# Attention in a two-layer graph network: scores and values on four 64x64 tiles, a new order of the pieces, channel means by DMA

## The chip, the cores and the metric

One core of a Trainium2 chip. The metric is the device time of one execution in microseconds (us), the median over several runs. All runs quoted here of one kernel lie within 0.2% of each other. In profiles PE is TensorE, PEld its weight loads, DVE is VectorE, ACT is ScalarE, POOL is GpSimd; L569 is a line of the kernel.

## The reference, cut to what matters

The first layer (a normalised graph product and two dense layers) is untouched by the change. The second layer is this, for 16 batches of 1024 nodes, 256 channels and 4 heads, all float32:

```python
c_adj = mean(x, channels)                      # one number per node
A   = 2 * | |sigmoid(c_j - c_i) - 0.5| - 0.5 |
g   = relu((x^T @ (adj * A)) * para)           # the queries q
k, v = x @ kv_w                                # 4 heads of 64 channels
attn = softmax(q k^T * scale)
out  = layernorm(x + attn @ v)
```

Of the kernel before, what the change touches and what calls it, by code (L numbers as in the profile page):

```python
# [9 lines left out]
F32 = mybir.dt.float32  # L10
# [3 lines left out]
PSUM = bass.MemoryType.PSUM  # L14
DRAM = bass.MemoryType.DRAM

P = 128
# [5 lines left out]
def gnn_norm_attention_kernel(  # L23
# [16 lines left out]
    nc = tc.nc  # L40
    B, N, C = x.shape
    H = W1.shape[0]
    NT = N // P
    CT = C // P
    HT = H // P
    FB = 512
    NH = N // FB
    HD = C // HEADS
# [3 lines left out]
    dram = ctx.enter_context(tc.tile_pool(name="dram", bufs=1, space=DRAM))  # L52
    ctx.enter_context(tc.manual_schedule())

    ident = const.tile([P, P], F32, name="ident")
# [22 lines left out]
    yT_all = dram.tile([B, P, CT, N], F32, name="yT")  # L78
    yT_dram = [yT_all[b] for b in range(B)]

    LDP = 2
    s2 = const.tile([P, CT], F32, name="s2")
    t2 = const.tile([P, CT], F32, name="t2")
# [2 lines left out]
    with ExitStack() as l0:  # L86
# [29 lines left out]
        with ExitStack() as ph1:  # L116
# [9 lines left out]
            for i in range(0, NT, 2):  # L126
                t = hp.tile([P, 2, N], F32, tag="h", name=f"A{i}")
# [29 lines left out]
            for h in range(NH):  # L157
# [11 lines left out]
                for j in range(NT):  # L169
                    p = ps.tile([P, FB], F32, tag="ah"[j % 2], name="pat")  # L170
# [25 lines left out]
            for c in range(HT):  # L196
                p = ps.tile([P, FB], F32, tag="a", name="pw1")
# [3 lines left out]
            for c in range(CT):  # L201
                p = ps.tile([P, FB], F32, tag="a", name="pw2")
# [90 lines left out]
            for b in range(B + 1):  # L293
                if b < B:
                    aggregate(b)
                if b > 0:
                    for h in range(NH):
                        u = (b - 1) * NH + h
                        hT[u] = hp.tile([P, HT, FB], F32, tag="h", name=f"hT{u}")
                        for f in range(HT):  # L300
                            p = hidden(b - 1, h, f)
# [34 lines left out]
        with ExitStack() as ph2:  # L336
# [3 lines left out]
            order = list(range(len(units) - KEEP, len(units))) + list(range(len(units) - KEEP))  # L340
# [68 lines left out]
    def fast():  # L409
      with ExitStack() as fx:  # L410
        pool = lambda name, bufs, **k: fx.enter_context(tc.tile_pool(name=name, bufs=bufs, **k))
        x1p = pool("x1p", 11)
        x1Tp = pool("x1Tp", 1)
        crp = pool("crp", 1)
# [8 lines left out]
        rp = pool("rp", 2)  # L423
        ps_s = pool("ps_s", 2, space=PSUM)
        ps_o = pool("ps_o", 1, space=PSUM)
        ps_t = pool("ps_t", 3, space=PSUM)

        x1s, x1Ts, css, crows, mvs, wgs = {}, {}, {}, {}, {}, {}
        kTs, qTs, vs, S, E, ACC, O, OT, DT = {}, {}, {}, {}, {}, {}, {}, {}, {}
# [44 lines left out]
            hcs[b] = sm.tile([P, NT], F32, tag="hcs", bufs=2, name=f"hcs_{b}")  # L474
            nc.vector.tensor_scalar_mul(hcs[b], css[b], 0.5)

        def crow(b, h):

            if h == 0:
                crows[b] = crp.tile([P, N], F32, tag="crow", name=f"crow_{b}")  # L480
            p = ps_t.tile([P, FB], F32, tag="t", name="pc")
            for k in range(FB // P):
                j = h * (FB // P) + k
                nc.tensor.transpose(p[:, ts(k, P)], css[b][:, j : j + 1].to_broadcast([P, P]), ident)
            nc.scalar.copy(crows[b][:, ts(h, FB)], p)


        def wg_a(b, i):
# [53 lines left out]
                nc.vector.tensor_scalar(qs, qs, 0.0, scale, op0=OP.max, op1=OP.mult)  # L542


        def step(g):
            b, s = divmod(g, NS)
            hf, pair, cp = s // (NP * NT // 2), s // (NT // 2) % NP, s % (NT // 2)
            return b, hf, pair, cp

        def scores(g):  # L550
            b, hf, pair, cp = step(g)
            for a in range(2):
                cb = 2 * cp + a
                t = ps_s.tile([P, 2, FB], F32, tag="s", name=f"s{g}_{a}")
                for h in range(2):
                    nc.tensor.matmul(  # L556
                        t[:, h, :],
                        kTs[b, pair][h * HD : (h + 1) * HD, ts(cb, P)],
                        qTs[b, pair, hf][h * HD : (h + 1) * HD, :],
                        start=True,  # L560
                        stop=True,
                    )
                S[g, a] = t

        def exps(g):
            for a in range(2):
                E[g, a] = ep.tile([P, 2, FB], F32, tag="e", name=f"e{g}_{a}")
                nc.scalar.activation(E[g, a], S.pop((g, a)), AF.Exp)  # L568

        def sums(g):  # L570
            b, hf, pair, cp = step(g)
            if cp == 0:
                ACC[b, hf, pair] = accp.tile([P, 2, FB], F32, tag="acc", name=f"acc{g}")
                nc.vector.tensor_add(ACC[b, hf, pair], E[g, 0], E[g, 1])  # L574
            else:
                for a in range(2):
                    nc.vector.tensor_add(ACC[b, hf, pair], ACC[b, hf, pair], E[g, a])  # L577

        def attend(g):
            b, hf, pair, cp = step(g)  # L580
            if cp == 0:
                O[b, hf, pair] = ps_o.tile([P, FB], F32, tag="o", name=f"o{g}")
            for a in range(2):
                cb = 2 * cp + a
                for h in range(2):
                    nc.tensor.matmul(  # L586
                        O[b, hf, pair][h * HD : (h + 1) * HD, :],
                        vs[b][:, cb, pair * P + h * HD : pair * P + (h + 1) * HD],
                        E[g, a][:, h, :],
                        start=(cb == 0),  # L590
                        stop=(cb == NT - 1),
                    )
                E.pop((g, a))
            if cp == NT // 2 - 1:
                t = otp.tile([P, FB], F32, tag=f"ot{pair}", bufs=2 - pair, name=f"ot{g}")
                nc.scalar.copy(t, O.pop((b, hf, pair)))
                OT[b, hf, pair] = t

        def dens(b, hf):
# [82 lines left out]
        NC = NS // 2  # L682
        at = {}

        def put(w, t, f, *a):
            at.setdefault(w * NC + t, []).append((f, a))

        WG = (3, 3, 1, 1)
        KV = (3, 3, 2)
        QG = (6, 6, 6, 7, 7)  # L690
        for b in range(B):

            for hf in range(NH):
                t = (hf + 1) * (NC // NH)
                put(b, t, dens, b, hf)
                put(b, t + 1, recips, b, hf)
                for k in range(KB // 2):
                    put(b, t + 1 + k, finish_a, b, hf * (KB // 2) + k)
                    put(b, t + 2 + k, finish_b, b, hf * (KB // 2) + k)

            put(b - 2, 2, begin, b)
            for j in range(NT // 2):
                if b > 0 or j >= LDP:
                    put(b - 2, j, load, b, j)
                put(b - 2, j + 1, bn2, b, j)
                put(b - 2, j + 2, ln1_a, b, j)
                put(b - 2, j + 3, ln1_b, b, j)
                put(b - 2, j + 4, x1_t, b, j)
            put(b - 2, NC - 2, means, b)
            for h in range(NH):  # L710
                put(b - 2, NC - 1, crow, b, h)

            i = 0
            for t, n in enumerate(WG):
                for i in range(i, i + n):
                    put(b - 1, t, wg_a, b, i)
                    put(b - 1, t, wg_b, b, i)
                i += 1
            kv = [(keys, (b, c, h)) for c in range(CT) for h in range(NH)]
            kv += [(values, (b, j)) for j in range(0, NT, 2)]  # L720
            for t, n in enumerate(KV):
                for _ in range(n):
                    f, a = kv.pop(0)
                    put(b - 1, t, f, *a)
            m = 0
            for t, n in enumerate(QG):
                for m in range(m, m + n):
                    put(b - 1, NC - len(QG) + t, graph, b, m)
                m += 1
# [3 lines left out]
        nsteps = B * NS  # L733
# [3 lines left out]
        rank = {f: k for k, f in enumerate(order)}  # L737
        short = (dens, recips, finish_a, x1_t, ln1_a, crow)
        long = (keys, values, graph)

        def arrange(pieces):
            few = sorted((fa for fa in pieces if fa[0] not in long), key=lambda fa: rank.get(fa[0], 11))
            many = [fa for fa in pieces if fa[0] in long]
            n = sum(f in short for f, _ in few)
            res, k, done = [], 0, 0
            for f, a in few:
                res.append((f, a))
                if f in short and f is not dens:
                    k += 1
                    upto = len(many) * k // n  # L750
                    res += many[done:upto]
                    done = upto
            return res + many[done:]

        for t in range(min(at), max(max(at), nsteps // 2 - 1) + 1):
            g = 2 * t
            now = arrange(at.get(t, []))
            live = [k for k in (g, g + 1) if 0 <= k < nsteps]
            ahead = [k for k in (g + 2, g + 3) if 0 <= k < nsteps]
            if ahead:  # L760
                scores(g + 2)
                exps(g + 2)
            while now and now[0][0] is dens:
                f, a = now.pop(0)
                f(*a)
            if live:
                sums(g)
            if not now and live:
                attend(g)
                live.pop(0)  # L770
                sums(g + 1)
            for f, a in now:
                f(*a)
            if now and live:
                sums(g + 1)
            if ahead:
                scores(g + 3)
                exps(g + 3)
            for k in live:
                attend(k)  # L780

        return nc.values_load(
            badi[0][0:1, 0:1],
# [3 lines left out]
        )  # L787

    flag = fast()


# [149 lines left out]
```

## The kernel before: the parts that the change touches

The second layer is one software pipeline. A batch has eight *turns* of two *steps*. A turn scores two steps (`s`, then exps on ScalarE), multiplies two earlier steps with the values (`o`), and between them does *pieces* that finish the batch before (`pd`, `pr`, `pf`), prepare the next (gate rows `wg`, keys `pk`, values `pv`, queries `pg`) and normalise the one after (`py`, `px`, means `pc`).

```python
ps_s = pool("ps_s", 2, space=PSUM)     # two tiles of two banks for scores
ps_o = pool("ps_o", 1, space=PSUM)     # one bank
ps_t = pool("ps_t", 3, space=PSUM)     # three banks for all the short-lived tiles
...
def scores(g):                         # 64 rows x 128 columns, two row tiles
    for h in range(2):
        nc.tensor.matmul(t[:, h, :], kTs[b, pair][h*HD:(h+1)*HD, ts(cb, P)],
                         qTs[b, pair, hf][h*HD:(h+1)*HD, :], start=True, stop=True)
def attend(g):                         # 128 rows x 64 columns, two column tiles
    for h in range(2):
        nc.tensor.matmul(O[h*HD:(h+1)*HD, :], vs[b][:, cb, ...64 columns...],
                         E[g, a][:, h, :], start=(cb == 0), stop=(cb == NT - 1))
def crow(b, h):                        # means of all nodes along every partition
    for k in range(FB // P):
        nc.tensor.transpose(p[:, ts(k, P)], css[b][:, j:j+1].to_broadcast([P, P]), ident)
    nc.scalar.copy(crows[b][:, ts(h, FB)], p)
... (cut)
for t in turns:                        # the order within a turn
    scores(g + 2); exps(g + 2)
    sums(g)                            # softmax denominators, VectorE
    for f, a in now: f(*a)             # the pieces
    sums(g + 1)
    scores(g + 3); exps(g + 3)
    attend(g); attend(g + 1)
```

## Time and profile before

| | before |
|---|---|
| time, median | 2702.65 us |
| TensorE busy | 97% of the span |
| VectorE, ScalarE busy | 51%, 45% |
| one batch in steady state | 113.03 us |
| waits of TensorE in it | 2.0 us |

"Busy" of TensorE includes the modelled tails of pipelined matmuls (593 ns for one of pg, where the next starts 0.43 us after it), so it hides the cost of a change of tile shape. What shows it is the distance from the start of one run of matmuls to the start of the next.

### The profile page before, as it was taken

To read this page: it belongs to the slowest core of one execution; us is meant where nothing else is said; L and a number is where in the kernel's file an instruction comes from. 1 tells how busy PE (TensorE), PEld (TensorE's weight loads), DVE (VectorE), ACT (ScalarE), POOL (GpSimd) and SP (SyncE) were. 2 spreads that over 40 slices of the span, in tenths; PEclk is the share of its full clock that TensorE was granted. 3 is DMA by queue.
4 is the path that set the end of the run, shared out by engine and by line. 5 is a ranking of instruction groups with operands and counts; after the bars stand their busy time and mean duration, and the time that the engine had idled before them with its cause. 6 is when DMAs were issued, how large, how long until landed. Compare 5 with 4: busy or idle time off the path is not lost.

```text
span 2701.5 us, 24578 instructions
## 1 busy us (share of the span) xinstructions
PE 2632.3 (97%) x9186; PEld 1127.8 (42%) x9186; DVE 1386.3 (51%) x2198; ACT 1223.3 (45%) x1650; POOL 259.5 (10%) x464
## 2 busy tenths in 40 slices
PE   8999999999998999999999999999999999999997
PEld 4444444444443444443444444344444443444432
DVE  5222222223213465665656656576565765657646
ACT  2111111114554555464554645546455464654634
POOL 1110111100000000100101001010000100001002
PEclk9999999999998999999999999999999999999999
DMA  3222122122863100010000100001000010000000
GB/s 125 94 78 78 78 94 88 72 106 93 319 218 109 32 16 24 28 43 24 24 24 28 43 24 24 24 28 43 24 24 24 28 43 24 24 24 28 12 8 25
DMA packets 91389, 153.18 MB, mean 57 GB/s; under 512 B 7296, under 2 KB 73344, under 8 KB 84352
## 3 DMA queue, kind: packets, MB, share of 16 engines
q1 hardware_dynamic: 91264, 151.55, 16.0%
q8 instruction: 74, 1.21, 0.2%
q14 instruction: 51, 0.42, 0.1%
HBM read 89.66 MB, written 61.87 MB: 56 GB/s over the span
## 4 chain that ended last, share of the span: by engine, by line
PE 90%; DVE 5%; ACT 3%; issue 1%; POOL 0%; DMA 0%; SPq 0%; ACTq 0%; DVEq 0%; POOLq 0%
PE s L556 16%; PE pg L536 16%; PE o L586 15%; PE pa L262 13%; PE po L360 8%; PE ph L283 8%; PE pk L510 4%; PE pv L521 3%; DVE wg L502 1%; PE px L469 1%; PE pd L605 1%; PE pa L246 1%; PE py L446 1%; PE pf L627 1%; DVE acc L577 1%
## 5 line engine op out<-in xcount | busy, mean ns | idle before, releaser
L568 ACT ACTIVATE e<-s 128x1024 f32<-128x1024 f32 x512 | 497.7, 1021 | 599.6 <-PE o L586 351.7
L556 PE MATMUL s<-qT,kT 64*128 64x512 f32 x2048 | 509.7, 616 | 17.4 <-ACT e L568 17.4
L577 DVE TENSOR_TENSOR acc<-acc,e 128x1024 f32<-128x1024 f32 x384 | 469.7, 1223 | 19.6 <-DVE acc L577 1.4
L536 PE MATMUL pg<-wg,x 128*128 128x512 f32 x1024 | 470.3, 593 | 0.6 <-DVE wg L502 0.6
L586 PE MATMUL o<-e,v 128*64 128x512 f32 x2048 | 467.7, 598 | 0.0
L556 PEld LDWEIGHTS s<-qT,kT 64*128 64x128 f32 x2048 | 174.8, 186 | 327.2 <-issue 192.2
L302 ACT COPY hT<-ph 128x512 f32<-128x512 f32 x128 | 75.0, 586 | 453.7 <-PE ph L283 453.7
L586 PEld LDWEIGHTS o<-e,v 128*64 128x64 f32 x2048 | 135.5, 136 | 316.5 <-issue 315.4
L536 PEld LDWEIGHTS pg<-wg,x 128*128 128x128 f32 x1024 | 180.2, 190 | 160.6 <-issue 159.2
L283 PE MATMUL ph<-agg,W1T 128*128 128x512 f32 x512 | 222.2, 592 | 0.0
L502 DVE SCALAR_TENSOR_TENSOR wg<-wg,adj_sb 128x1024 f32<-128x1024 f32 x128 | 156.8, 1225 | 77.4 <-ACT wg L498 73.9
L360 PE MATMUL po<-hL,W2T 128*128 128x512 f32 x432 | 185.6, 592 | 0.0
L303 DVE BATCH_NORM_STATS2 st<-ph 128x6 f32<-128x512 f32 x128 | 89.5, 699 | 136.6 <-ACT hT L302 136.6
L262 PE MATMUL pa<-T,sx 128*128 128x512 f32 x360 | 156.9, 592 | 0.0
L574 DVE TENSOR_TENSOR acc<-e,e 128x1024 f32<-128x1024 f32 x64 | 78.2, 1222 | 153.0 <-PE pd L605 153.0
L283 PEld LDWEIGHTS ph<-agg,W1T 128*128 128x128 f32 x512 | 97.3, 190 | 122.5 <-issue 122.2
L541 DVE TENSOR_TENSOR qT<-pg,para_sb 128x512 f32<-128x512 f32 x64 | 44.2, 691 | 203.0 <-PE pg L536 203.0
L66 POOL TENSOR_SCALAR rs_z<-mv_z 128x2 f32<-128x2 f32 x64 | 17.5, 274 | 1194.1 <-DVE mv_z L401 1041.6
L364 DVE BATCH_NORM_STATS2 st<-po 128x6 f32<-128x512 f32 x64 | 44.8, 699 | 169.3 <-PE po L360 169.3
L521 PE MATMUL pv<-kvw,x1T 128*128 128x256 f32 x512 | 119.4, 382 | 6.6 <-DVE r L630 6.6
L360 PEld LDWEIGHTS po<-hL,W2T 128*128 128x128 f32 x432 | 82.1, 190 | 103.3 <-issue 103.3
L510 PE MATMUL pk<-x1T,kvw 128*128 128x512 f32 x256 | 117.8, 603 | 0.6 <-ACT kT L513 0.6
(130 smaller groups left out, 2450.5 us busy)
## 6 DMA issues: line engine op xcount, KB each, us to landing
h<-hT SPq DMA_DIRECT2D x27, 1024.0 KB, 3.8
hL<-h SPq DMA_DIRECT2D x27, 1024.0 KB, 6.2
x<-in_x_dram SPq DMA_DIRECT2D x16, 1024.0 KB, 5.2
yT<-y SPq DMA_DIRECT2D x32, 512.0 KB, 3.7
yt<-yT SPq DMA_DIRECT2D x64, 256.0 KB, 3.6
xr<-in_x_dram SPq DMA_DIRECT2D x64, 256.0 KB, 3.6
out_dram<-r SPq DMA_DIRECT2D x64, 256.0 KB, 2.1
A<-in_adj_dram SPq DMA_DIRECT2D x4, 1024.0 KB, 7.9
```

The lines of the kernel that those rows point to most:

```text
L262: nc.tensor.matmul(p, w[:, k, :], m[:, k, :], start=(k == 0), stop=(k == KN - 1))
L283: nc.tensor.matmul(p, W1T[:, k, ts(f, P)], aggT[b][:, k, ts(h, FB)], start=(k == 0), stop=(k == CT - 1),)
L303: nc.vector.bn_stats(st1[:, f, u, :], p)
L360: nc.tensor.matmul(po[c], W2T[:, k, ts(c, P)], hT[u][:, k, :], start=(k == 0), stop=(k == HT - 1))
L502: nc.vector.scalar_tensor_tensor(t, t, 1.0, adj_sb[:, i, :], op0=OP.add, op1=OP.mult)
L510: nc.tensor.matmul(p, kvw[:, k, ts(c, P)], x1Ts[b][:, k, ts(h, FB)], start=(k == 0), stop=(k == CT - 1))
L521: nc.tensor.matmul(p[:, ts(a, C)], x1Ts[b][:, k, ts(j + a, P)], kvw[:, k, C:], start=(k == 0), stop=(k == CT - 1),)
L536: nc.tensor.matmul(pg[b], x1s[b, k // 2][:, k % 2, ts(c, P)], wgs[b, k][:, ts(h, FB)], start=(k == 0), stop=(k == NT - 1))
L556: nc.tensor.matmul(t[:, h, :], kTs[b, pair][h * HD : (h + 1) * HD, ts(cb, P)], qTs[b, pair, hf][h * HD : (h + 1) * HD, :], start=True, sto ...
L568: nc.scalar.activation(E[g, a], S.pop((g, a)), AF.Exp)
L577: nc.vector.tensor_add(ACC[b, hf, pair], ACC[b, hf, pair], E[g, a])
L586: nc.tensor.matmul(O[b, hf, pair][h * HD : (h + 1) * HD, :], vs[b][:, cb, pair * P + h * HD : pair * P + (h + 1) * HD], E[g, a][:, h, :], ...
```

## The change

Its intent: 64x64 tiles let scores and values share one tile shape, so that a turn can run s, o, s, o as one stretch without the *edges* between shapes. (An edge is the time that TensorE loses when a run of matmuls in one tile shape follows a run in another, 0.14 to 0.20 us in the kernel before; a *slot* is the 0.43 us from one 128x128 matmul of 512 columns to the next.) For this, each pair of products becomes four small ones, o takes two PSUM banks, one for each row tile, and the short-lived tiles lose a bank. The turn is reordered: pieces first, then s, o, s, o; sums behind the last short piece; two gate rows in each of four turns; pieces spread among each other. Scores now run one step less ahead of the values that use them. The channel means go out to memory and come back broadcast.

```diff
-        ps_t = pool("ps_t", 3, space=PSUM)
+        ps_t = pool("ps_t", 2, space=PSUM)
 ... crow
+            nc.tensor.transpose(p[:NT, :P], css[b], ident)
+            t = crows[b][:NT, :P]
+            nc.scalar.copy(t, p[:NT, :P])
+            nc.sync.dma_start(c_dram[b], t)
+            nc.sync.dma_start(crows[b], c_dram[b].rearrange("j p -> (j p)").partition_broadcast(P))
 ... scores (attend alike, with row tile r into bank r of o)
+                for r in range(2):
+                    for h in range(2):
+                        nc.tensor.matmul(t[r * HD : (r + 1) * HD, h, :],
+                            kTs[b, pair][h * HD : (h + 1) * HD, ts(2 * cb + r, HD)],
+                            qTs[b, pair, hf][h * HD : (h + 1) * HD, :], start=True, stop=True)
 ... end of attend
+                nc.scalar.copy(t, o[:, 0, :])
+                nc.vector.tensor_add(t, o[:, 1, :], t)
 ...
-        WG = (3, 3, 1, 1)
+        WG = (2, 2, 2, 2)
 ... arrange: pieces spread among each other (cut); the turn:
+            for k in range(len(now) + 1):
+                if k == behind and g in live:
+                    sums(g)
+                if k < len(now):
+                    f, a = now[k]; f(*a)
+            for k in (g, g + 1):
+                if k + 1 in ahead:
+                    scores(k + 1); exps(k + 1)
+                if k in live:
+                    if k > g: sums(k)
+                    attend(k)
```

More of the change, by code (lines that the diff above doesn't have):

```diff
@@ L79, in gnn_norm_attention_kernel @@
     yT_dram = [yT_all[b] for b in range(B)]
+    c_dram = [dram.tile([NT, P], F32, name=f"crow_d{b}") for b in range(B)]
     LDP = 2
@@ L475, in means, with crow @@
             nc.vector.tensor_scalar_mul(hcs[b], css[b], 0.5)
-        def crow(b, h):
-            if h == 0:
-                crows[b] = crp.tile([P, N], F32, tag="crow", name=f"crow_{b}")
-            p = ps_t.tile([P, FB], F32, tag="t", name="pc")
-            for k in range(FB // P):
-                j = h * (FB // P) + k
-                nc.tensor.transpose(p[:, ts(k, P)], css[b][:, j : j + 1].to_broadcast([P, P]), ident)
-            nc.scalar.copy(crows[b][:, ts(h, FB)], p)
+        def crow(b):
+            crows[b] = crp.tile([P, N], F32, tag="crow", name=f"crow_{b}")
+            if b == 0:
+                for h in range(NH):
+                    p = ps_t.tile([P, FB], F32, tag="t", name="pc")
+                    for k in range(FB // P):
+                        j = h * (FB // P) + k
+                        nc.tensor.transpose(p[:, ts(k, P)], css[b][:, j : j + 1].to_broadcast([P, P]), ident)
+                    nc.scalar.copy(crows[b][:, ts(h, FB)], p)
+                return
+            p = ps_t.tile([P, FB], F32, tag="t", name="pc")
+            nc.tensor.transpose(p[:NT, :P], css[b], ident)
[3 more added lines that the diff above has]
+            nc.sync.dma_start(crows[b], c_dram[b].rearrange("j p -> (j p)").partition_broadcast(P))
         def wg_a(b, i):
@@ L554, in scores @@
                 t = ps_s.tile([P, 2, FB], F32, tag="s", name=f"s{g}_{a}")
-                for h in range(2):
-                    nc.tensor.matmul(
-                        t[:, h, :],
-                        kTs[b, pair][h * HD : (h + 1) * HD, ts(cb, P)],
-                        qTs[b, pair, hf][h * HD : (h + 1) * HD, :],
-                        start=True,
-                        stop=True,
-                    )
+                for r in range(2):
+                    for h in range(2):
+                        nc.tensor.matmul(
+                            t[r * HD : (r + 1) * HD, h, :],
+                            kTs[b, pair][h * HD : (h + 1) * HD, ts(2 * cb + r, HD)],
+                            qTs[b, pair, hf][h * HD : (h + 1) * HD, :],
+                            start=True,
+                            stop=True,
+                        )
                 S[g, a] = t
@@ L581, in attend @@
             if cp == 0:
-                O[b, hf, pair] = ps_o.tile([P, FB], F32, tag="o", name=f"o{g}")
+                O[b, hf, pair] = ps_o.tile([P, 2, FB], F32, tag="o", name=f"o{g}")
             for a in range(2):
                 cb = 2 * cp + a
-                for h in range(2):
-                    nc.tensor.matmul(
-                        O[b, hf, pair][h * HD : (h + 1) * HD, :],
-                        vs[b][:, cb, pair * P + h * HD : pair * P + (h + 1) * HD],
-                        E[g, a][:, h, :],
-                        start=(cb == 0),
-                        stop=(cb == NT - 1),
-                    )
+                for r in range(2):
+                    for h in range(2):
+                        nc.tensor.matmul(
+                            O[b, hf, pair][h * HD : (h + 1) * HD, r, :],
+                            vs[b][r * HD : (r + 1) * HD, cb, pair * P + h * HD : pair * P + (h + 1) * HD],
+                            E[g, a][r * HD : (r + 1) * HD, h, :],
+                            start=(cb == 0),
+                            stop=(cb == NT - 1),
+                        )
                 E.pop((g, a))
@@ L595, in attend @@
                 t = otp.tile([P, FB], F32, tag=f"ot{pair}", bufs=2 - pair, name=f"ot{g}")
-                nc.scalar.copy(t, O.pop((b, hf, pair)))
+                o = O.pop((b, hf, pair))
+                nc.scalar.copy(t, o[:, 0, :])
+                nc.vector.tensor_add(t, o[:, 1, :], t)
                 OT[b, hf, pair] = t
@@ L709, in fast @@
             put(b - 2, NC - 2, means, b)
-            for h in range(NH):
-                put(b - 2, NC - 1, crow, b, h)
+            put(b - 2, NC - 1, crow, b)
             i = 0
@@ L739, in fast, with spread @@
         long = (keys, values, graph)
+        def spread(few, many):
+            res, done = [], 0
+            for k, fa in enumerate(few):
+                upto = len(many) * (k + 1) // (len(few) + 1)
+                res += many[done:upto] + [fa]
+                done = upto
+            return res + many[done:]
         def arrange(pieces):
-            few = sorted((fa for fa in pieces if fa[0] not in long), key=lambda fa: rank.get(fa[0], 11))
+            first = [fa for fa in pieces if fa[0] is dens]
+            gate = [fa for fa in pieces if fa[0] in (wg_a, wg_b)]
             many = [fa for fa in pieces if fa[0] in long]
-            n = sum(f in short for f, _ in few)
-            res, k, done = [], 0, 0
-            for f, a in few:
-                res.append((f, a))
-                if f in short and f is not dens:
-                    k += 1
-                    upto = len(many) * k // n
-                    res += many[done:upto]
-                    done = upto
-            return res + many[done:]
+            few = [fa for fa in pieces if fa not in first + gate + many]
+            few.sort(key=lambda fa: rank.get(fa[0], len(rank)))
+            few_pe = [fa for fa in few if fa[0] in short]
+            order = spread(many, few_pe) if len(many) < len(few_pe) else spread(few_pe, many)
+            if few_pe and many and order[0][0] in long:
+                order.remove(few_pe[0])
+                order.insert(0, few_pe[0])
+            for fa in few:
+                if fa[0] not in short:
+                    at_ = 0
+                    for k, o in enumerate(order):
+                        if o[0] in rank and rank[o[0]] <= rank.get(fa[0], len(rank)):
+                            at_ = k + 1
+                    order.insert(at_, fa)
+            pairs = [gate[k : k + 2] for k in range(0, len(gate), 2)]
+            res = spread(order, pairs) if order else pairs
+            flat = []
+            for o in res:
+                flat += o if isinstance(o, list) else [o]
+            return first + flat
         for t in range(min(at), max(max(at), nsteps // 2 - 1) + 1):
@@ L758, in fast @@
             live = [k for k in (g, g + 1) if 0 <= k < nsteps]
-            ahead = [k for k in (g + 2, g + 3) if 0 <= k < nsteps]
-            if ahead:
-                scores(g + 2)
-                exps(g + 2)
-            while now and now[0][0] is dens:
-                f, a = now.pop(0)
-                f(*a)
-            if live:
-                sums(g)
-            if not now and live:
-                attend(g)
-                live.pop(0)
-                sums(g + 1)
-            for f, a in now:
-                f(*a)
-            if now and live:
-                sums(g + 1)
-            if ahead:
-                scores(g + 3)
-                exps(g + 3)
-            for k in live:
-                attend(k)
+            ahead = [k for k in (g + 1, g + 2) if 0 <= k < nsteps]
+            behind = max((k + 1 for k, fa in enumerate(now) if fa[0] in short), default=0)
+            for k in range(len(now) + 1):
+                if k == behind and g in live:
+                    sums(g)
+                if k < len(now):
+                    f, a = now[k]
+                    f(*a)
+            for k in (g, g + 1):
+                if k + 1 in ahead:
+                    scores(k + 1)
+                    exps(k + 1)
+                if k in live:
+                    if k > g:
+                        sums(k)
+                    attend(k)
         return nc.values_load(
```

## The prediction

> **What bounds the kernel now.** I read the page first, then the table of groups, the timeline of TensorE alone for one batch, and the waits. The second layer's first scores start at 926 us; the first layer (0 to 926) is not touched by the change. The page says that TensorE is the bound:
>
> ```profile
> PE 2632.3 (97%) x9186; PEld 1127.8 (42%) x9186; DVE 1386.3 (51%) x2198; ACT 1223.3 (45%) x1650; POOL 259.5 (10%) x464
> ...
> PE 90%; DVE 5%; ACT 3%; issue 1%; POOL 0%; DMA 0%; SPq 0%; ACTq 0%; DVEq 0%; POOLq 0%
> ...
> L556 PE MATMUL s<-qT,kT 64*128 64x512 f32 x2048 | 509.7, 616 | 17.4 <-ACT e L568 17.4
> L577 DVE TENSOR_TENSOR acc<-acc,e 128x1024 f32<-128x1024 f32 x384 | 469.7, 1223 | 19.6 <-DVE acc L577 1.4
> L536 PE MATMUL pg<-wg,x 128*128 128x512 f32 x1024 | 470.3, 593 | 0.6 <-DVE wg L502 0.6
> L586 PE MATMUL o<-e,v 128*64 128x512 f32 x2048 | 467.7, 598 | 0.0
> ```
>
> The chain is 90% TensorE, so only time on TensorE, or a new wait of it, counts. Scores run as 64*128 (two row tiles), values as 128*64 (two column tiles), all else as 128*128 or 128*32. The groups' busy times hide what a change of shape costs, because the modelled tails overlap; start times do not. Here is the timeline of TensorE in turns 1 and 2 of a batch (columns: start, length, work, idle before it):
>
> ```profile
> 1512.55 1.99 PE L556 MATMUL s<-qT,kT 64*128 64x512 f32 x8
> 1514.47 0.66 PE L616 MATMUL pr<-ident,dt 128*128 128x128 f32 x4
> 1514.96 1.88 PE L510 MATMUL pk<-x1T,kvw 128*128 128x512 f32 x4
> 1516.68 0.60 PE L627 MATMUL pf<-ident,ot 128*128 128x128 f32 x4
> 1517.12 3.62 PE L521 MATMUL pv<-kvw,x1T 128*128 128x256 f32 x16
> 1520.67 1.99 PE L556 MATMUL s<-qT,kT 64*128 64x512 f32 x8
> 1522.59 3.65 PE L586 MATMUL o<-e,v 128*64 128x512 f32 x16
> 1527.52 2.05 PE L556 MATMUL s<-qT,kT 64*128 64x512 f32 x8 [1.28 <-ACT e L568]
> 1529.50 0.66 PE L627 MATMUL pf<-ident,ot 128*128 128x128 f32 x4
> 1529.99 1.89 PE L521 MATMUL pv<-kvw,x1T 128*128 128x256 f32 x8
> 1531.72 0.60 PE L446 MATMUL py<-ident,yt 128*128 128x128 f32 x4
> 1532.82 1.99 PE L521 MATMUL pv<-kvw,x1T 128*128 128x256 f32 x8 [0.50 <-DVE r L630]
> ```
>
> Start to start: four pk matmuls take 1516.68-1514.96 = 1.72, so 0.43 us each; that is the steady slot. Eight s records are four concurrent pairs, ideally 4 x 0.43 = 1.72, but 1514.47-1512.55 = 1.92: 0.20 more. Sixteen o records are eight pairs, ideally 3.44; undisturbed they take 3.58 (1508.97 to 1512.55): 0.14 more. So a run in another tile shape costs 0.14 (64 columns of weights) to 0.20 us (128 columns). A turn has four such edges: s, pieces, s, o, then s again. A batch is eight turns and 113.03 us (pd starts at 1500.71 and again at 1613.74). Two waits of TensorE recur in each batch: the second s above starts 1.35 late (1522.59 to 1527.52 is 4.93, not 3.58), and pv about 0.67 late (py takes 1.10, not 0.44): 2.0 us a batch, 30 us over 15 batches.
>
> [...] 0.52 instead of 0.43 from the last matmul of one shape to the next shape, and the first load is exposed. [...] The trace shows it for two tiles (pairs in one 0.43 slot) and for pd's four column tiles (eight records in 0.99), not for a long stream of four-tile groups. [...] at 1533 pv waits for a VectorE product that stood behind sums.
>
> **The change part by part.**
>
> *Tiles.* Four 64*64 products fill the array as two 64*128 did: still 8 slots of scores and 8 of values a turn, twice the records. If four tiles share a slot, the core s,o,s,o takes 16 x 0.43 = 6.87 + one exit 0.09 + one entry 0.05 to 0.1 = 7.03. Before: 1.92 + 1.92 + 3.58 = 7.42. Saved 0.39 to 0.40 a turn, x 128 turns = **51 us**.
>
> *Channel means.* Before, two pc pieces of 0.44 a batch; after, one narrow transposition with two changes of shape (about 0.35 to 0.4): saved 0.5 x 15 = **7 us** of TensorE, and two copies of 0.586 to one small one on ScalarE. The two transfers (4 KB out, broadcast in) start in turn 7, about 10 us before the first gate row needs them; 256 KB loads here land in 3.6 us, so this is hidden.
>
> *Second half of o.* 64 additions on VectorE of 0.69 (from the 128x512 additions out of PSUM, 691 ns): 44 us of VectorE, 0.7 in every second turn. It stands after the copy, ahead of the next pieces' work.
>
> *Buffers.* o takes a bank from the short-lived PSUM tiles: three become two. One is held by pg through turns 3 to 7, so then there is one for everything else.
>
> *Order.* From the lists in the change I wrote out the pieces: turn 1 is pr, pk, pv, gate row 2, pf, pv, gate row 3; turn 2 is pf, pv, py, row 4, pv, row 5; turn 3 py, row 6, six pg, row 7; turn 4 pd, px, pg..., py; turn 5 pr, pg, pg, pf, pg, px, pg, py, pg, pg. The sums follow the last short piece. The exps are behind the pieces.
>
> I then followed the queues by hand. VectorE lengths: one sum 1.25 (four in 5.00), even gate row 1.23, odd row 0.72+1.23, pf's work 2.6, py's 1.9. ScalarE: exp 0.97, copy 0.53 to 0.59, even row 2.13, odd 1.04.
> Turn 1 (time from its first piece): pk copied 2.95, pv copied 4.65, row 2 done on ScalarE at 6.9. VectorE was idle from 0.9 until then, as the row's product stands ahead of pf. From 6.9: row 1.25, pf 2.6, two sums 2.5, row 3 1.95, two sums 2.5, o addition 0.7: ends at 18.4. The turn lasts 6.2 + 7.05, plus some 0.7 (pv waits for a copy; exps late) = 14.0. VectorE enters turn 2 with 4.4 us of backlog.
> Turn 2: pf takes one buffer, pv the other, and py needs pf's, free at 4.4 + 0.7 = 5.1 rather than 2.2: **2.9 us** lost. The three buffers of before lost 0.67 at this place.
> Turn 3: no loss; VectorE catches up to within a microsecond.
> Turn 4: px needs pd's buffer while pg holds the other, a copy's latency: **0.75**. Turn 5: the second pg needs a buffer that its predecessor's product frees only after pf's statistics: **0.9**.
> Sum 0.7 + 2.9 + 0.75 + 0.9 = 5.3 a batch, x 15 = **80 us**.
>
> Total by this count: 2703 - 51 - 7 - 30 (old waits gone) + 80 = 2695.
>
> **The rivals.** (a) *The new order hides all waits.* Then 2703 - 51 - 7 - 30 = 2615 plus a few, about 2620. For it: sums stand behind the evacuations now, ScalarE is no longer given three gate rows in turn 1, and VectorE is busy only 70.9 of 113.03 us of a batch. Against: turns 1 to 3 hold most of its work, in order. (b) *The two PSUM buffers take back the gain*, as counted: 2690 to 2700. For it: the old order already waited with three buffers, and 2.6 us of VectorE backlog was there. Against: my count hangs on which buffer is taken; if py takes pv's, turn 2 loses 0.75 and the total is about 2662. (c) *Four tiles don't stream at 0.43.* Eight instructions per slot; at 0.50 a group this adds 0.07 x 16 x 128 = 143 us: about 2840 at worst. Against: four transpositions with their loads, also eight instructions, take 0.44 here. Weight loads of 64 columns take 0.137 and fit even if two go in turn.
>
> **Range and chances.** The count says 2695; the changed order looks made to avoid such waits, and half of my 80 us rests on one buffer. I take 2680 as the middle, between (b) and its milder form. The low end 2630 is near (a); the high end 2712 is (b) with waits I did not see. Faster by over 2% means under 2649: 0.27, mostly (a). Slower by over 2% means over 2757: 0.05, all (c). Within: 0.68.
>
> **What would show it.** Timeline of TensorE: s,o,s,o as one stretch of 7.0 to 7.05 us without gaps at the three inner edges confirms the tiles; a 0.52 step between s and o, or slots over 0.43, refutes it. Idle of 2 to 3 us before py in turn 2, ended by VectorE's r product (L630's counterpart), confirms (b); none there means (a). TensorE's waits on VectorE and ScalarE should sum to 60 to 90 us, against 24 before (17.4 for s, 6.6 for pv). The wait of s for exp should fall from 17.4 to under 8. Gate rows should not wait for a transfer; if they do, the hidden-transfer step is wrong.

"The trace shows it" means that several tiles share a slot. That o has a bank for each row tile is how the change is written.

## The result, and the profile after

The changed kernel takes **2692.79 us** (2689.07 to 2693.58, four runs), 9.9 us less. The ratio is 0.996 (95% interval 0.9943 to 0.9977); ratios are the mean time of one kernel's fast runs over that of the other's of the same rounds, so not quite the ratio of the medians. The class "within 2%" and the range held; the size did not: 22.8 us were forecast, 9.9 came.

The page after, with the lines that answer to those of before (busy us, mean ns, idle before):

```profile
PE 2593.2 (96%) x13177; PEld 1109.3 (41%) x13177; DVE 1420.8 (53%) x2262; ACT 1215.7 (45%) x1635; POOL 415.5 (15%) x464
...
PE 88%; DVE 8%; ACT 2%; issue 2%; DMA 0%; POOL 0%; SPq 0%; DVEq 0%; ACTq 0%; POOLq 0%
...
L590 DVE TENSOR_TENSOR acc<-acc,e 128x1024 f32<-128x1024 f32 x384 | 469.1, 1222 | 83.2 <-ACT e L581 62.8
L569 PE MATMUL s<-qT,kT 64*64 64x512 f32 x4096 | 493.4, 597 | 0.0
L600 PE MATMUL o<-e,v 64*64 64x512 f32 x4096 | 485.4, 589 | 0.0
L546 PE MATMUL pg<-wg,x 128*128 128x512 f32 x1024 | 468.8, 595 | 9.7 <-DVE qT L551 8.0
```

VectorE's share of the chain that ended last has gone from 5% to 8%: TensorE did less and waited more. The timeline of TensorE in turns 1 and 2 of a batch shows both (start, length, work, idle before it and what ended it):

```profile
1508.16 0.66 PE L632 MATMUL pr<-ident,dt 128*128 128x128 f32 x4
...
1510.37 1.89 PE L531 MATMUL pv<-kvw,x1T 128*128 128x256 f32 x8
1512.10 0.60 PE L643 MATMUL pf<-ident,ot 128*128 128x128 f32 x4
1512.94 1.99 PE L531 MATMUL pv<-kvw,x1T 128*128 128x256 f32 x8 [0.24 <-ACT v L538]
...
1522.13 0.66 PE L643 MATMUL pf<-ident,ot 128*128 128x128 f32 x4
1522.63 1.89 PE L531 MATMUL pv<-kvw,x1T 128*128 128x256 f32 x8
1526.79 0.65 PE L447 MATMUL py<-ident,yt 128*128 128x128 f32 x4 [2.27 <-DVE r L646]
1527.28 1.89 PE L531 MATMUL pv<-kvw,x1T 128*128 128x256 f32 x8
1529.11 1.95 PE L569 MATMUL s<-qT,kT 64*64 64x512 f32 x16
1530.87 1.90 PE L600 MATMUL o<-e,v 64*64 64x512 f32 x16
1532.59 1.90 PE L569 MATMUL s<-qT,kT 64*64 64x512 f32 x16
1534.31 1.90 PE L600 MATMUL o<-e,v 64*64 64x512 f32 x16
1536.13 0.66 PE L447 MATMUL py<-ident,yt 128*128 128x128 f32 x4
```

The tiles do what they should: from s at 1529.11 to the next piece at 1536.13 is 7.02 us, and s to o is 1.72, four slots of 0.43, with no edge. But py in turn 2 starts 1526.79 - 1522.63 = 4.16 us after pv, which takes 1.73 where nothing waits (1512.10 - 1510.37): 2.4 us are lost there, and VectorE's product r ended it. Two more waits recur, in turns 4 and 5:

```profile
1550.67 0.66 PE L470 MATMUL px<-ident,x 128*128 128x128 f32 x4 [0.71 <-ACT dt L623]
...
1569.98 1.98 PE L546 MATMUL pg<-wg,x 128*128 128x512 f32 x4 [0.52 <-DVE qT L551]
```

Why VectorE was late is in the timeline of all engines, same turns, cut to VectorE's path:

```profile
1512.30 0.59 ACT L538 COPY v<-pv 128x512 f32<-128x512 f32 x1 [1.14 <-PE pv L531]
1512.78 1.15 ACT L507 ACTIVATE wg<-crow,cs 128x1024 f32<-128x1024 f32 x1
...
1513.97 1.06 ACT L508 ACTIVATE wg<-wg 128x1024 f32<-128x1024 f32 x1
...
1515.06 1.23 DVE L512 SCALAR_TENSOR_TENSOR wg<-wg,adj_sb 128x1024 f32<-128x1024 f32 x1 [5.94 <-ACT wg L508]
...
1516.20 0.68 DVE L646 TENSOR_TENSOR r<-pf,RD 128x512 f32<-128x512 f32 x1
...
1522.96 2.57 DVE L590 TENSOR_TENSOR acc<-acc,e 128x1024 f32<-128x1024 f32 x2
...
1526.06 0.68 DVE L646 TENSOR_TENSOR r<-pf,RD 128x512 f32<-128x512 f32 x1
```

pf of turn 1 was ready on TensorE at 1512.7, but VectorE stood idle for 5.94 us before a gate row's product that was queued ahead of it, and took up pf at 1516.20. All the sums slid back by that, so that pf of turn 2, ready at 1522.8, was taken up at 1526.06, and py got its buffer then.

A second thing was not in the prediction at all. Of 13 steady batches seven last 111.93 us and six 113.5 to 113.6 us. In the long ones, the turn with the long wait goes on at a lower clock. This is the table of windows, 3.7 us from py in two neighbouring batches (length; busy time of PE, PEld, DVE, ACT and POOL; PEclk; DMA share; GB/s):

```profile
1526.79:1530.50 3.71, 3.71 (x28) 2.40 (x32) 3.50 (x11) 3.42 (x6) 1.44 (x4) 1.00 0.32 99
1638.73:1642.50 3.77, 3.77 (x12) 3.03 (x12) 3.56 (x11) 2.12 (x4) 1.45 (x5) 0.58 0.31 101
```

The granted clock is 0.58 in the second. The trace's clock record has six such episodes of 3.41 us at half rate in the steady state, and none there in the kernel before; each costs 1.55 to 1.69 us.

### The profile page after: what moved, and what is told of

Read it like the earlier page. It is cut to its first block, busy times and chain, and to the rows that moved or that the text cites. A ratio compares the mean times of both kernels' runs of the same rounds, so it can differ in the third digit from the quotient of the medians.

```text
span 2690.7 us, 32816 instructions
## 1 busy us (share of the span) xinstructions
PE 2593.2 (96%) x13177; PEld 1109.3 (41%) x13177; DVE 1420.8 (53%) x2262; ACT 1215.7 (45%) x1635; POOL 415.5 (15%) x464
## 3 DMA queue, kind: packets, MB, share of 16 engines
q8 instruction: 105, 1.72, 0.3%
## 4 chain that ended last, share of the span: by engine, by line
PE 88%; DVE 8%; ACT 2%; issue 2%; DMA 0%; POOL 0%; SPq 0%; DVEq 0%; ACTq 0%; POOLq 0%
PE s L569 15%; PE pg L546 15%; PE o L600 15%; PE pa L263 13%; PE po L361 8%; PE ph L284 8%; PE pk L520 4%; PE pv L531 3%; DVE acc L590 2%; PE pd L621 1%; PE py L447 1%; PE px L470 1%; DVE r L646 1%; PE pa L247 1%; DVE st_z L401 1%
## 5 line engine op out<-in xcount | busy, mean ns | idle before, releaser
L569 PE MATMUL s<-qT,kT 64*64 64x512 f32 x4096 | 493.4, 597 | 0.0
L600 PE MATMUL o<-e,v 64*64 64x512 f32 x4096 | 485.4, 589 | 0.0
L600 PEld LDWEIGHTS o<-e,v 64*64 64x64 f32 x4096 | 156.4, 133 | 283.1 <-issue 281.5
L569 PEld LDWEIGHTS s<-qT,kT 64*64 64x64 f32 x4096 | 141.4, 132 | 300.4 <-issue 271.9
L66 POOL TENSOR_SCALAR rs_z<-mv_z 128x2 f32<-128x2 f32 x64 | 43.5, 680 | 1054.1 <-DVE mv_z L402 1053.1
L531 PE MATMUL pv<-kvw,x1T 128*128 128x256 f32 x512 | 130.4, 401 | 7.8 <-ACT v L538 4.5
L66 POOL TENSOR_SCALAR rs_a<-mv_a 128x2 f32<-128x2 f32 x64 | 63.0, 984 | 419.5 <-DVE mv_a L402 419.5
```

What stands on the lines that cost most here:

```text
L66: nc.gpsimd.tensor_scalar(dst, src, add, None, op0=OP.add)
L531: nc.tensor.matmul(p[:, ts(a, C)], x1Ts[b][:, k, ts(j + a, P)], kvw[:, k, C:], start=(k == 0), stop=(k == CT - 1),)
L569: nc.tensor.matmul(t[r * HD : (r + 1) * HD, h, :], kTs[b, pair][h * HD : (h + 1) * HD, ts(2 * cb + r, HD)], qTs[b, pair, hf][h * HD : (h + ...
L600: nc.tensor.matmul(O[b, hf, pair][h * HD : (h + 1) * HD, r, :], vs[b][r * HD : (r + 1) * HD, cb, pair * P + h * HD : pair * P + (h + 1) * HD],
```

## The experiments

Eleven kernels ran, all timed in three rounds against the kernel before on the same chip; its median was 2702.4 to 2702.7 in each. Theory: the tiles save their edges, and most of that is paid back in waits that come from two PSUM buffers instead of three *and* from VectorE's order in turn 1; the idle time also lowers the clock. Rivals: the tiles save nothing; only the buffers matter; only the order matters.

### e1: the old tile shapes in the new kernel

```diff
-  four 64x64 products in scores and in attend, o in two banks, addition of its halves
+  two 64x128 products in scores, two 128x64 in attend, o in one bank (as before)
```

> The changed kernel with its order, its DMA means and its two short-lived PSUM buffers, but scores as 64x128 and values as 128x64 in one bank, as before the change. Theory (the four 64x64 tiles save the edges between shapes, but VectorE gives part back as waits): the stretch s,o,s,o grows from 7.03 to about 7.54 us, 0.5 x 128 = 65 us; the longer turn and the missing o addition shorten VectorE's backlog, so py in turn 2 waits about 1.3 us instead of 2.4, and the clock keeps full rate: about 2730 us. Rival (the tiles save nothing because VectorE sets the pace anyway): within 10 us of the changed kernel's 2693.

Measured: 2736.54 us, ratio 1.0128. A batch takes 115.13 us, py waits 1.37 us, the clock record shows no half-rate episode in the steady state (mean granted clock 0.994, as in the kernel before, against 0.990 in the changed one). So the tiles save 2736.5 - 2692.8 = 44 us here: the rival that they save nothing falls. In the traces the stretch s, o, s, o takes 7.57 us here and 7.03 in the changed kernel, so the edges are worth 0.54 x 128 = 69 us. The rest is paid back: py in turn 2 loses 2.43 us instead of 1.53, as VectorE has less time in a shorter turn, and s in turn 1 comes 0.24 late, in some 14 batches 16 us together; the half-rate clock takes 8 (e11).

### e2: the old shapes and the third buffer

```diff
 (e1)
-        ps_t = pool("ps_t", 2, space=PSUM)
+        ps_t = pool("ps_t", 3, space=PSUM)
```

> As e1, with the third short-lived PSUM buffer given back. Theory (two of the four new waits are for the missing buffer): the waits of px in turn 4 (0.78 us) and of pg in turn 5 (0.69) and the 0.4 in turn 1 go, some of turn 2 stays because VectorE is late: 15 x 1.8 = 27 us less than e1, about 2703. Rival (the waits come from the order on VectorE alone, buffers are innocent): same as e1 within 8 us.

Measured: 2703.01 us, ratio 1.0001. The waits of turns 1, 4 and 5 (before pv, px and pg) are gone. That of turn 2 is not; it stands before pv now. The timeline of TensorE:

```profile
1523.77 0.66 PE L639 MATMUL pf<-ident,ot 128*128 128x128 f32 x4
...
1527.63 1.99 PE L531 MATMUL pv<-kvw,x1T 128*128 128x256 f32 x8 [1.04 <-DVE r L642]
1529.56 1.99 PE L568 MATMUL s<-qT,kT 64*128 64x512 f32 x8
```

From pf to s turn 2 takes 5.79 us here, 6.07 in e1, and 4.48 in e10 where nothing waits; and s of turn 1 now comes 0.40 late for its exps, which it does not in e1. So the bank that o takes costs 2736.5 - 2703.0 = 33.5 us in this order, but through turns 1, 4 and 5: a third buffer hardly helps turn 2 while VectorE is late.

### e3: one swap on VectorE in turn 1

```diff
             for k in range(len(flat) - 1):
+                if flat[k][0] is wg_b and flat[k + 1][0] is finish_a:
+                    flat[k], flat[k + 1] = flat[k + 1], flat[k]
```

> The changed kernel, only the product of gate row 2 with adj goes behind pf's work on VectorE in turn 1 (one swap in the order). Theory (VectorE stands idle for 6 us in turn 1 because that product waits for ScalarE, and this idle time comes back as 2.4 us of wait of py in turn 2): pf's work starts about 3.5 us earlier, py's wait falls to about 1.2 us, and the half-rate clock episodes after it (6 of 15 batches, 1.67 us each) disappear: about 2663 us. Rival (the buffers alone cause it): py waits as before, 2690.

Measured: 2659.66 us, ratio 0.9839: 33 us less than the changed kernel, with two buffers as there. The timeline of TensorE in turn 2:

```profile
1512.96 0.66 PE L643 MATMUL pf<-ident,ot 128*128 128x128 f32 x4
1513.45 1.89 PE L531 MATMUL pv<-kvw,x1T 128*128 128x256 f32 x8
1515.35 0.66 PE L447 MATMUL py<-ident,yt 128*128 128x128 f32 x4
```

py starts 1.90 after pv instead of 4.16, so 0.17 of its wait is left where I had expected 1.2, and all batches last 110.19 us at full clock (0.994 in the mean over the run, as before the change). (The pv after py and the s of turn 2 come 0.23 and 0.24 late in its place, and are part of that time.) So the wait of turn 2 comes from VectorE's order: with two buffers a better order removes it, while in e2 a third buffer without that order leaves most of it. The waits of turns 1, 4 and 5 are the ones that the missing buffer makes in this order (e2). (The 64x64 tiles with three buffers were not run.)

### e4: VectorE relieved (wrong result)

```diff
-                for a in range(2):
-                    nc.vector.tensor_add(ACC[b, hf, pair], ACC[b, hf, pair], E[g, a])
+                pass
```

> The changed kernel with six of every seven softmax sums left out (the result is wrong on purpose): 384 additions of 1.22 us leave VectorE, nothing else changes. Theory: with no backlog on VectorE the wait of py in turn 2 (2.5 us) and the half-rate clock go, while the waits for a copy or for a product in order (0.4 in turn 1, 0.78 in turn 4, 0.69 in turn 5) stay: 15 x 2.5 + 10 = 48 us less than the changed kernel, about 2645 us. Rival (the wait is one for the buffer whatever VectorE does): 2685 or more.

Measured: 2659.23 us; the result is wrong as intended. py's wait and the half-rate clock are gone (granted clock 0.994 in the mean), so VectorE's backlog is their cause. The gain is 33.6 us, not 48: pv after py now loses 0.40 us to ScalarE's copy and s of turn 2 comes 0.24 late, both hidden by py's wait before, and the half-rate clock costs 8 rather than 10 (e11). e3 reaches the same time without taking any work from VectorE.

### e5: the channel means alone, in the kernel before

```diff
-            for h in range(NH): put(b - 2, NC - 1, crow, b, h)
+            put(b - 2, NC - 1, crow, b)          # with crow as in the change
```

> The kernel before with the channel means by DMA alone. Theory: eight transpositions (0.88 us a batch) become one of 0.11 without an edge, as the trace after shows it, 0.77 x 15 = 11.5 us less: 2691 us. Rival (gate rows then wait for the transfer, or the waits of turn 1 absorb it): 2700 or more.

Measured: 2691.25 us, ratio 0.9957. By itself this smallest part gives 11 us, as much as the whole change. The narrow transposition costs no edge: pc starts at 1597.32 and the next pg at 1597.43, 0.11 us later, as after px in the kernel before.

### e6: two pieces moved in turns 4 and 5

```diff
 (e3)
+   4: pd, pg, px, pg, pg, pg, py, ...              # was pd, px, pg, pg, pg, pg, py, ...
+   5: pr, pg, pf, pg, pg, px, pg, pg, py, pg       # was pr, pg, pg, pf, pg, px, pg, py, pg, pg
```

> e3 with two more swaps of the order: a product pg stands between pd and px in turn 4, and in turn 5 pf comes one pg earlier and py one pg later. Theory: the waits of 0.78 and 0.69 us are for one buffer's evacuation and are hidden behind TensorE work of 0.86 us: 15 x 1.4 = 21 us less than e3's 2660, about 2638. Rival (the waits move elsewhere, as ScalarE and VectorE set the pace of a batch): 2655 or more.

Measured: 2639.10 us, ratio 0.9763. Both waits are gone; they do not come back elsewhere.

### e7: turn 1 in another order as well

```diff
 (e6)
+   1: pr, pf, pk, gate row, pv, pv, gate row       # was pr, pk, pv, gate row, pf, pv, gate row
```

> e6 with turn 1 in another order as well: pr, pf, pk, gate row 2, pv, pv, gate row 3, so that VectorE starts pf's work at once and no long piece follows the next but one too early for its buffer. Theory: the waits in turn 1 (0.4) and the small ones of turn 2 (0.2 to 0.4) go: 15 x 0.6 = 9 us less than e6, about 2630. Rival: ScalarE, late with its exps in turn 1, takes it back: as e6.

Measured: 2631.69 us (2630.50 to 2632.08), ratio 0.9737, 95% interval 0.9721 to 0.9753, result correct. **It beats both kernels**, with a batch at 108.16 us. The timeline of TensorE shows the only wait that it marks in turns 1 and 2, and turn 4 without one:

```profile
1503.32 1.99 PE L531 MATMUL pv<-kvw,x1T 128*128 128x256 f32 x8 [0.24 <-ACT v L538]
...
1525.28 1.06 PE L621 MATMUL pd<-acc,ones 128*32 128x512 f32 x8
1526.28 1.12 PE L546 MATMUL pg<-wg,x 128*128 128x512 f32 x2
1527.24 0.60 PE L470 MATMUL px<-ident,x 128*128 128x128 f32 x4
```

### e8: the tiles alone, in the order of before

```diff
 (before)
-  two products in scores and attend;  ps_t three buffers
+  four 64x64 products in each, o in two banks;  ps_t two buffers
```

> The kernel before with only the 64x64 tiles (two banks for o, so two short-lived PSUM buffers); the order of before, means by transposition. Theory: fewer edges save 0.25 us a turn, 32 us, as s and o stay apart in the turn except at its end; the missing buffer adds the waits of turns 4 and 5 (0.7 each) and about 1 us in turn 2: 15 x 2.4 = 36 us. About 2707. Rival (the new order alone makes the waits, the buffer does not matter): 2675.

Measured: 2797.67 us, ratio 1.035. My expectation missed by 90 us. In turn 0 the third pk needs the buffer of the first, whose copy stands on ScalarE behind three gate rows in a row (timeline of TensorE):

```profile
1547.56 3.00 PE L510 MATMUL pk<-x1T,kvw 128*128 128x512 f32 x4 [2.88 <-ACT kT L513]
```

The clock falls too: the granted clock is 0.985 in the mean, against 0.994 before, and after the wait shown s takes 2.40 us to the start of o (1550.49 to 1552.89) instead of 1.77 (1564.84 to 1566.61). So some 40 of the 95 us are this wait (2.88 x 14) and some 25 the clock (0.009 of 2797), both estimates; py waits another 1.59 us for VectorE in each batch, and pv, px and pg wait in smaller parts. I had read only the turns where VectorE evacuates. So with two buffers the new order is not decoration: without it the tiles lose 95 us. What the spread gate rows alone give was not run.

### e9 and e10: the order of e7 with the old shapes, two and three buffers

```diff
 (e7)
-  64x64 tiles, o in two banks
+  old shapes, o in one bank          # e9; e10 also ps_t = pool("ps_t", 3, ...)
```

> e7's order with the tile shapes of before (64x128 and 128x64, o in one bank), still two short-lived PSUM buffers. Theory: with the waits out of the way the 64x64 tiles are worth their full 0.51 us a turn, 65 us: e7's 2632 + 65 = 2697 us, more than the 44 us that separate e1 from the changed kernel. Rival: the tiles are worth 44 us in any order: 2676.

Measured: 2696.81 us, ratio 0.998. Against e7 the tiles are worth 65.1 us. The number was met, but by two parts: the stretch is 0.54 us shorter (7.57 to 7.03), 69 us in 128 turns, and e7 loses 0.24 a batch where s of turn 2 comes late. In the order of the change the tiles were worth 44.

> e9 with three short-lived PSUM buffers. Theory: in e7's order the third buffer is worth no more than the 0.4 us a batch that pv still waits in turn 2: 6 us less than e9, about 2691. Rival (the buffer is worth as much in any order): 33 us less, as e2 against e1.

Measured: 2686.07 us, ratio 0.9939. The third buffer is worth 10.7 us in this order, against 33.5 in that of the change. Of these, 6.5 are the 0.50 us by which each of 13 batches is shorter; 2.5 lie before these batches and 1.5 after them, which I had not counted.

### e11: the wait filled with useless work

```diff
+        def fill(b):
+            t = ps_s.tile([P, 2, FB], F32, tag="s", name=f"fill{b}")
+            for i in range(2):
+                nc.tensor.matmul(t[:, i, :], kvw[:, 0, :P], adj_sb[:, 0, :FB], start=True, stop=True)
 ... ahead of py in turn 2 of the changed kernel
```

> The changed kernel with two products that nobody reads (1.72 us of TensorE work into a free scores buffer) ahead of py in turn 2, inside its wait of 2.4 us for VectorE. Theory: the wait stays as long, but TensorE is idle for 0.7 us instead of 2.3, so the granted clock no longer falls to half for 3.41 us in 6 of the batches: the periods are all 111.93 us and the time is 10 us less than the changed kernel, about 2683. Rival (the half-rate episodes have another cause): 2693, and the episodes stay.

Measured: 2684.42 us, ratio 0.9933. The timeline of TensorE:

```profile
1520.47 1.89 PE L536 MATMUL pv<-kvw,x1T 128*128 128x256 f32 x8
1522.20 1.88 PE L528 MATMUL fill<-adj_sb,kvw 128*128 128x512 f32 x4
1524.63 0.66 PE L447 MATMUL py<-ident,yt 128*128 128x128 f32 x4 [0.55 <-DVE r L651]
```

py still comes 4.16 us after pv, the wait for VectorE is unchanged, but all batches last 111.93 us and the half-rate episodes are gone (granted clock 0.994 in the mean, against 0.990 in the changed kernel): 8.4 us for doing work that nobody reads. So the idle time of TensorE is what lowered the clock here; which batches it did so in is sorted out after the points on the prediction.

### The runs together

| tiles | order | short-lived buffers | us |
|---|---|---|---|
| old | before | 3 (before) | 2702.65 |
| old | before, means by DMA | 3 (e5) | 2691.25 |
| 64x64 | before | 2 (e8) | 2797.67 |
| old | of the change | 3 (e2) | 2703.01 |
| old | of the change | 2 (e1) | 2736.54 |
| 64x64 | of the change | 2 (the change) | 2692.79 |
| 64x64 | of the change, wait filled | 2 (e11) | 2684.42 |
| 64x64 | of the change, sums left out (wrong result) | 2 (e4) | 2659.23 |
| 64x64 | one swap on VectorE | 2 (e3) | 2659.66 |
| 64x64 | of e6 | 2 (e6) | 2639.10 |
| old | of e7 | 3 (e10) | 2686.07 |
| old | of e7 | 2 (e9) | 2696.81 |
| 64x64 | of e7 | 2 (e7) | 2631.69 |

So, taken in these steps, the 9.9 us are: means -11 (e5), order with old shapes +12 (e2 against e5), loss of a buffer +33.5 (e1 against e2), tiles -44 (the change against e1). The shares depend on the path: in e7's order the same tiles are worth 65 us and the buffer 10.7. The order alone costs 12 because s, o, s, o with two shapes has one edge more than s, pieces, s, o, o: 7.57 us in the traces of e1, e2 and e9 against 7.42 before, 0.15 x 128 = 19 us. Some 7 of these come back, as e2 loses 1.7 us a batch in waits and the kernel before 2.2 (see below).

## Why the prediction was wrong in size, point by point

- **Tiles, 51 us.** Right. The core s, o, s, o is 7.02 to 7.03 us as counted (7.27 in turn 1, where s waits); four fp32 tiles share a 0.43 slot through 64 records. Rival (c) is refuted.
- **Means, 7 us.** Right in kind, low in size: I gave the narrow transposition 0.35 to 0.4 us, with two changes of shape; it takes 0.11. 11 us (e5). The transfers are hidden: the broadcast lands 3.8 us after its issue, and no gate row waits for one.
- **Old waits gone, 2.0 us a batch.** Right: neither of the two is left as it was. By the reading of the next point they cost 2.2 (1.4 for s, 0.8 before pv).
- **New waits, 5.3 us a batch.** The places and causes were all right. What a turn loses is the time from its first piece to its s, less what the same pieces take where nothing waits (turn 2 in e10, the others in e2): turn 1 6.70 - 6.19, and 0.24 in its stretch, 0.75 (counted 0.7); turn 2 6.98 - 4.48 = 2.50 (2.9); turn 4 7.95 - 7.18 = 0.77 (0.75); turn 5 8.02 - 7.05 = 0.97 (0.9). That is 5.0 a batch, and it closes the sum: 3.1 + 0.8 + 2.2 saved less 5.0 is 1.1, and an undisturbed batch is 1.10 shorter. The waits recur in about 14 batches (13 for py, 16 for pg), not 15: some 70 us (an estimate), not 80.
- **The clock.** Missing. I counted a wait as its own length only. Six times it was followed by 3.41 us at half clock, 8.4 us in all by e11's time, 9.9 by the long batches of the trace.
- **The failing step** is in "Range and chances": "The count says 2695; the changed order looks made to avoid such waits, and half of my 80 us rests on one buffer. I take 2680 as the middle". This took the new waits at 65 us instead of the 80 counted, and no view of the profile spoke for these 15 us: the order had been followed already in the count, and the buffer was the one I had assumed. The runs showed some 70 us of waits and 8.4 of half clock after them, 78 together, so the count's own 2695 stood beside the 2692.8 measured.
- **What was luck in the count.** Its waits were some 10 us too long, and the clock, which it did not have, took 8 of these. And where it forecast 0.3 us a batch in 15 equal batches (5.6 - 5.3), the 13 steady ones save 0.35 on average (1.10, less 1.55 to 1.69 in six of them), 4.5 us of the 10.8 by which the profiled spans differ. The other 6.3 lie before these batches (4.9) and after them (1.4); no run isolates that part.
- **Its signs.** The stretch has no gap at its inner edges, the wait of s fell from 17.4 us to 0.0, py's wait of 2.27 is ended by r, and no gate row waits for a transfer: all as listed. Only the waits of TensorE in the table of waits sum to 52 us (py 29.5, px 9.9, pg 8.0, pv 4.5) and not to 60 to 90; that table counts idle time from the modelled ends and shows less than the distances between starts.
- **Rival (a)** (all waits hidden, 2620) is not this kernel, but it exists: e7 at 2632 has the same tiles, buffers and means, with three turns in another order. **Rival (b)** was the case in time, but it blames the two buffers alone; half of its 80 us, the wait of turn 2, is VectorE's order (e2, e3).

Which of the equal waits are followed by half clock can be sorted by the clock record of the changed kernel. Its six episodes start whole multiples of 3.413 us apart (66, 66, 99, 66 and 66). Cut the trace into stretches of that length, counted from these starts. In the six batches with an episode, the stretch just before it held 2.05 to 2.27 us of TensorE's idle time. In the seven others the wait of 2.27 us lay across two stretches, the fuller with 1.21 to 1.92 us, and the record shows the full clock. In the steady batches of the kernel before, cut likewise by its own record, no stretch held more than 1.28 us, and none fell to half clock. This sorts 13 waits of one trace and is no rule: the idle times are those of the modelled ends, how the chip sets its clock is not shown, and no run shifts a wait on purpose.

What stays open: the 6.3 us of the gain that lie outside the 13 steady batches.

## What to carry to other kernels

When a change shortens the bounding engine's path, count what it does to the engines that release its buffers: edges worth 69 us came out as 44, because VectorE, which stood idle for 6 us a batch behind a product whose input was late, held TensorE up for longer, and because the clock fell after six of these waits (8.4 us by e11). One buffer fewer added waits elsewhere, 33.5 us in this order and 10.7 in a better one. VectorE took its queue in order here (r, whose pf was ready at 1512.7, came at 1516.20, behind a product that waited 5.94 us for ScalarE). With such a queue, put the instruction that frees a buffer ahead of one that waits for another engine; one such swap gave 33 us here, three turns so ordered 61. Add to the cost of a wait what the clock does after it (1.55 to 1.69 us in six batches here), and do not discount a count by how well-made a change looks.

## What else the traces show

- In the kernel before an edge costs 0.09 us on the way out (0.52 from the last matmul of one shape to the next run, instead of the slot of 0.43) and, from the 3.58 us of o's eight slots and the 1.92 of s's four, 0.05 (64 columns of weights) to 0.11 (128 columns) on the way in. A stationary operand of 8 columns (pc, shown as 128*8, in e5) cost none: the matmul after it started 0.11 us later, as after px in the kernel before. The long stream of 64x64 fp32 tiles in the changed kernel keeps the slot at 0.43 us: 64 records, four to a slot, in 7.02 to 7.03 us with the edges at its ends.
- In the changed kernel 2.27 us of wait were enough in 6 of 13 batches for 3.41 us at half clock: those with 2.05 us or more in one stretch of the sorting above. With the gap at 0.55 (e11) the granted clock was 0.994 in the mean, as in the kernel before.
- The addition into rs_a on GpSimd took 292 ns on average before, where none of 64 overlaps a softmax sum of VectorE, and 984 after, where 56 of 64 do (1063 ns on average), each ending 75 to 80 ns after the sum; the other eight took 435. Why it is so is not shown. TensorE did not wait for it. The group of before, in the table of groups:

```profile
L66 POOL TENSOR_SCALAR rs_a<-mv_a 128x2 f32<-128x2 f32 x64 | 18.7, 292 | 446.0 <-DVE mv_a L401 446.0
```

  The same group after:

```profile
L66 POOL TENSOR_SCALAR rs_a<-mv_a 128x2 f32<-128x2 f32 x64 | 63.0, 984 | 419.5 <-DVE mv_a L402 419.5
```
